# The half tile of a graph-attention layer as rows in pairs, and a neighbourhood-attention layer's projections spread evenly: one Trainium2 core

## The chip, the cores and the metric

The kernel runs as one program on one core of one Trainium2 chip. The metric is the device time of an execution in microseconds: the median of several runs, three for the kernel before.

## The reference, cut to what matters

The input is four images of 56 x 56 tokens with 256 channels, in float32. Four layers follow each other; each computes `x = x + layer(groupnorm(x))`. Layer 0 is attention of 8 heads over a 7 x 7 neighbourhood, layer 2 the same with two dilations and a position bias, layer 3 attention in shifted 7 x 7 windows. Layer 1 is attention of every token to every other of its image, with a kernel that is symmetric since `W_adj` is used by its diagonal:

```python
xn = x / jnp.maximum(jnp.linalg.norm(x, axis=-1, keepdims=True), EPS)
A = jnp.einsum('bnc,cc,bmc->bnm', xn, W_adj, xn)
A = jnp.exp(5.0 * (A - jnp.max(A, axis=-1, keepdims=True)))
A = A * (1.0 - jnp.eye(n, dtype=A.dtype))
A = A / jnp.maximum(jnp.sum(jnp.abs(A), axis=-1, keepdims=True), EPS)
rowsum = jnp.sum(A, axis=-1, keepdims=True)
xW = jnp.einsum('bnc,dc->bnd', x, W_aff)
AxW = jnp.einsum('bnc,dc->bnd', jnp.einsum('bnm,bmc->bnc', A, x), W_aff)
diff = rowsum * (xW + b_aff) - AxW      # then layer norm and leaky relu
```

An image has 3136 tokens, which is 24 tiles of 128 and a rest of 64.

## The kernel before, in words

The four layers run one after the other, each over all four images; activations stand in DRAM between them, with channels on partitions. [...] In layer 1 the order of PE's instructions is the order of the program; the order on the other engines there, and on all engines in layer 0, is made by the framework's scheduler.

**Layer 0** (`layer0`, L1139). An image is read in 7 chunks of 8 rows (448 tokens), so there are 28 chunks. `prepare` (L1173) normalises a chunk on DVE and issues a later chunk's load; `project_rows` (L1187) makes six steps of it: two of values (PE, eviction on DVE, then a store of v to DRAM by SP), two of keys and two of queries (PE, eviction on ACT). The attention goes in 32 blocks of 7 rows, each of four column tiles (`pair`, L1219): PE computes logits of 4 heads at a time on 32-row strips (L1071), DVE and POOL apply masks, ACT the exponential, POOL adds the two halves of the keys (L1091), PE multiplies by v and by ones on 32-column strips (L1100), and DVE divides. `project_out` (L1269) follows one block later. `stream` (L1282) hands out the waiting steps, seven a chunk (six of projection and one `prepare`), among the blocks: chunks 0 and 1 are projected before the first block (L1311 to L1317), and after block `r` a total of `min(182, (7 * (7 * r + 12)) // 8)` steps is done (L1295). All 182 are handed out by block 28.

**Layer 1** (`layer1`, L1331). The rest of 64 tokens is the 25th tile, filled with zeros to 128 (`NB` is 25, L1343 and L1344). `tokens` (L1346) prepares a chunk of up to four tiles: a load, normalising, lengths (PE, L1368), `xW` in `xw` (PE, L1381; with -1 in an added column, which yields the row sum), unit-length tokens in `xnT` (PE L1389, DVE L1391). As A is symmetric before it is divided, only tile pairs with `i >= j` are computed. A unit is row `j` and up to four tiles `i`: `logits` (PE L1409, one matmul of up to 512 columns for each half of the channels; exponential on ACT, L1412; POOL clears the diagonal, L1414), `transposed` (PE L1423 into `ps_t`, copy on ACT, L1426), `products`. There each tile gives a product by column into one of the two banks of `ps_v` (PE L1442), which DVE copies (row 0, L1444) or adds (L1446) to `acc[:, i]`, and a product by row, accumulated in PSUM, `ps_o` (PE L1437). An image has 91 units. After a row, `finish` (L1465) adds `acc` and `ps_o` and applies the layer norm with a chain of operations on DVE and POOL; its `add` (L1491) transposes the result on PE, adds it to the residual and stores a full chunk.

The main loop (L1545) emits for unit k: a small step, the transposes of k, the logits of k + 1, a small step, the products of k. Small steps are the parts of `tokens` for the next image and the `add`s, each due after a number of tiles. `replace` (L1539) starts a chunk of the next image as soon as its tiles are no longer used: chunks 0 to 4 at rows 6, 10, 14, 18 and 22, chunk 5 at row 24, chunk 6 (the rest) at row 0 of the next image. `there` (L1533) emits at once what the next logits need.

Of the kernel before, what the change touches and what calls it, by code (L numbers as in the profile page):

```python
# [830 lines left out]
def direct_blocks(ctx: ExitStack, tc: tile.TileContext, d: dict, watch):  # L831
# [307 lines left out]
    def layer0(early, big, pool, brief):  # L1139
# [142 lines left out]
        def stream():  # L1282
            n = NIMG * NCH
            rows = []
            for c in range(2, n):
                rows += lazily(project_rows, c, 6)
                rows.append(lambda c=c: prepare(c + 1) if c + 1 < n else None)
            look_at = {}
            for b in range(NIMG - 1):
                for i in range(NCH):  # L1290
                    look_at.setdefault(NB0 * b + min(i // 2 + (b == 0), 3), []).append((b + 1) * NCH + i)
            gone = 0
            for r in range(NIMG * NB0):
                b, g = divmod(r, NB0)
                to = min(len(rows), (7 * (7 * r + 12)) // 8)  # L1295
                steps, gone = rows[gone:to], to
                steps += [lambda i=i: first_look(i) for i in sorted(looks)]
                steps.append(lambda r=r: [load(i, looks, "xs") for i in look_at.get(r + 1, [])])
                for i in range(3 if g > 3 or g == 0 else 0):
                    steps.insert(2 * i, step_stats)  # L1300
                if r:
                    steps += table[:3]
                    if len(table) in (1, 2, 3):
                        steps.append(tables.close)
                    del table[:3]
                    at = (len(steps) + 1) // 2
                    steps[at:at] = project_out(r - 1)
                attns[r] = pool.tile([P, CC, BT], FP, tag="attn", name="attn0")
                yield from spread([pair(r, t) for t in range(NTC)], steps)

        for r in range(3):  # L1311
            prepare(r)
            if r == 0:
                load(3)
            if r < 2:
                for step in project_rows(r):
                    step()  # L1317
        check_sizes(pool)
        tables = ExitStack()
        both = [tables.enter_context(tc.tile_pool(name=f"t{n}", bufs=n, side="right", reuse_waits="tile")) for n in (1, 2)]  # L1320
# [7 lines left out]

    def layer1(early, big, pool, brief):  # L1331
        NB = -(-T // P)
        real = lambda i: min(P, T - i * P)
        nonlocal m_bufs
        m_bufs, ps_a = 1, ps_m
        w_aff = weight(early, "waff", C)
        acc = big.tile([P, NB, C + 1], FP, name="acc")
        xnT = big.tile([P, CC, NB * P], FP, name="xnT")
        xw = big.tile([P, NB, C + 1], FP, name="xw")
        offd = big.tile([P, P], FP, name="offd")  # L1340
        nc.vector.tensor_scalar(offd, ident, -1.0, 1.0, ALU.mult, ALU.add)
        nc.vector.memset(xw[:, :, C:], -1.0)
        nc.vector.memset(xw[T % P:, NB - 1, :], 0.0)  # L1343
        nc.vector.memset(xnT[:, :, T:], 0.0)  # L1344

        def tokens(b, c, ps_a=ps_m):  # L1346

            tiles = range(4 * c, min(4 * c + 4, NB))
            n = sum(real(t) for t in tiles)
            k, m = real(tiles[0]), len(tiles)  # L1350
            box = {}

            def load():
                x = early.tile([P, CC, 512], FP, tag="x", name="x1")
                nc.sync.dma_start(out=x[:, :, :n], in_=tokens_of(1, b, 4 * c * P, n))
                x1 = box["x"] = early.tile([P, CC, 512], FP, tag="xn", name="xn1")
                sq = box["sq"] = early.tile([P, CC, 512], FP, tag="sq", name="sq", bufs=1)
                for h in range(CC):
                    normalise(x1[:, h, :n], x[:, h, :n], known(1, b), h)
                nc.scalar.activation(sq[:, :, :n], x1[:, :, :n], AF.Square)  # L1360
# [25 lines left out]
            def unit_length():  # L1386

                pm = ps_a()
                nc.tensor.matmul(pm[:, :n].rearrange("p (m k) -> p m k", k=k), lhsT=ones[:k, :], rhs=box["dg"][:k, :m, :k],  # L1389
                                 start=True, stop=True)  # L1390
                nc.vector.tensor_tensor(xnT[:, :, 4 * c * P:4 * c * P + n], box["x"][:, :, :n],  # L1391
                                        pm[:, :n].rearrange("p (o k) -> p o k", o=1).to_broadcast([P, CC, n]), ALU.mult)

            return [load, lengths] + [lambda i=i: values(i) for i in range(0, m, 2)] + [unit_length]

        xd, out, xr = {}, {}, {}

        def scaled(j):

# [4 lines left out]
        def logits(b, j, first, last):  # L1404

            n = (last - first) * P
            s = psum_tile("s", 2)
            for h in range(CC):
                nc.tensor.matmul(s[:, :n], lhsT=xd[j][:, h, :], rhs=xnT[:, h, first * P:last * P],  # L1409
                                 start=(h == 0), stop=(h == CC - 1))  # L1410
            e = pool.tile([P, 512], FP, tag="e", name="e1", bufs=3)
            nc.scalar.activation(e[:, :n], s[:, :n], AF.Exp, scale=5.0)  # L1412
            if first == j:
                nc.gpsimd.tensor_tensor(e[:, :P], e[:, :P], offd, ALU.mult)  # L1414
            return e

        def transposed(b, j, first, last, e):
            at = pool.tile([P, 512], FP, tag="at", name="at1")
# [10 lines left out]
        def products(b, j, first, last, e, at):  # L1429
# [10 lines left out]
            def by_column(i):  # L1440
                pv = psum_tile("v", 2)
                nc.tensor.matmul(pv[:, :C + 1], lhsT=e[:, col(i)], rhs=xw[:, j, :], start=True, stop=True)  # L1442
                if j == 0:
                    nc.vector.tensor_copy(acc[:, i, :], pv[:, :C + 1])  # L1444
                else:
                    nc.vector.tensor_tensor(acc[:, i, :], acc[:, i, :], pv[:, :C + 1], ALU.add)  # L1446

            rows = list(range(first, last))
            if first == j:
# [5 lines left out]
            for i in rows:  # L1455
                by_row(i)

        def residual(b, c):

            if (b, c) not in xr and c < NCH:  # L1460
# [3 lines left out]

        def finish(b, j):  # L1465

            n = real(j)
            y = pool.tile([P, C + 1], FP, tag="y", name="y", bufs=5)
            u = pool.tile([P, C], FP, tag="u", name="u")
            rd = pool.tile([P, 1], FP, tag="rd", name="rd")  # L1470
            nc.gpsimd.tensor_tensor(u[:n], xw[:n, j, :C], baff[:n], ALU.add)
            if j:
                nc.vector.tensor_tensor(y[:n], out[j][:n, :C + 1], acc[:n, j, :], ALU.add)
            else:
                nc.vector.tensor_copy(y[:n], out[j][:n, :C + 1])
            nc.vector.reciprocal(rd[:n], y[:n, C:])
            y = y[:n, :C]
            nc.vector.scalar_tensor_tensor(y, y, rd[:n], u[:n], ALU.mult, ALU.add)
# [12 lines left out]
            def add():  # L1491
# [5 lines left out]
                while t0 < j * P + n:  # L1497
# [2 lines left out]
                    x = residual(b, c)  # L1500
                    xv = x[:, :, t0 - c * CH:t1 - c * CH]
                    nc.vector.tensor_tensor(xv, xv, pt[:, :, t0 - j * P:t1 - j * P], ALU.add)
                    if t1 == (c + 1) * CH:
                        add_stats(2, b, c, x)
                        nc.sync.dma_start(out=tokens_of(2, b, c * CH, CH), in_=x)
                    t0 = t1
# [1 line left out]

        NC4 = -(-NB // 4)
        units = [(b, j, i, min(i + 4, NB)) for b in range(NIMG) for j in range(NB) for i in range(j, NB, 4)]
        turn = iter(range(4 * NC4))
        fresh = [tokens(0, c, lambda: psum_tile(*(("v", 2), ("o", 2), ("t", 1), ("s", 2))[next(turn) % 4])) for c in range(NC4)]
        for c in range(2):
            fresh[c].pop(0)()
        for c in range(NC4):
            for step in fresh[c]:
                step()
            if c + 2 < NC4:  # L1520
                fresh[c + 2].pop(0)()
        scaled(0)
        e = logits(*units[0])
        small, done = [], 0

        def small_step():
# [3 lines left out]
                    return step()  # L1530
            step_stats()

        def there(b, tile):  # L1533

            for item in [a for a in small if a[2] == (b, tile // 4)]:
                small.remove(item)
                item[1]()

        def replace(b, c):  # L1539
            load, *steps = tokens(b, c)  # L1540
            load()
            at = sum(a[2] is not None for a in small)
            small[at:at] = [(done + 8, step, (b, c)) for step in steps]

        for k, w in enumerate(units):  # L1545
            b, j, first, last = w
            if first == j:
                residual(b, j * P // CH)
                residual(b, j * P // CH + 1)
                if b + 1 < NIMG and j % 4 == 2 and j >= 6:  # L1550
                    replace(b + 1, j // 4 - 1)
                if b + 1 < NIMG and j == NB - 1:
                    replace(b + 1, NC4 - 2)
                if b and j == 0:
                    replace(b, NC4 - 1)
            small_step()
            at = transposed(*w, e)
            if k + 2 < len(units) and units[k + 2][1] == units[k + 2][2]:
                scaled(units[k + 2][1])
            if k + 1 < len(units):  # L1560
                there(units[k + 1][0], units[k + 1][3] - 1)
                ahead = logits(*units[k + 1])
            small_step()
            products(*w, e, at)
            done += last - first
            if last == NB:
                small.append((done + 6, finish(b, j), None))
            e = ahead
        for _, step, _ in small:
            step()  # L1570
# [495 lines left out]
```

## Time and profile before

| what | us |
|---|---|
| median of 3 runs (4103.39 to 4105.45) | 4103.79 |
| the profiled execution's own time | 4092.52 |
| its span in the profile | 4090.7 |
| layer 0, to the first matmul of layer 1 | 0 to 809 |
| layer 1, to the first matmul of layer 2 | 809 to 2846 |
| layers 2 and 3 | 2846 to 4091 |
| PE busy | 3889.7 |
| DVE, POOL, ACT busy | 2369.5, 1741.9, 1377.7 |

The profile is of one execution. Its time is the span plus 1.8 us outside of it, and 11.3 us below the median of the runs. PE is TensorE, DVE VectorE, ACT ScalarE, POOL GpSimd, SP the engine that issues nearly all DMAs. A float32 matmul shows as two records. Records of PE overlap[...]; what one costs is the distance from start to start. "Granted clock" is the share of TensorE's full clock that it was given.

### The profile page before, as it was taken

What the parts mean: (1) busy time and instruction counts of PE and PEld (TensorE: products, weight loads), DVE (VectorE), ACT (ScalarE), POOL (GpSimd) and SP (SyncE); (2) the same over time, 40 slices, a digit from 0 to 9 for tenths busy, and PEclk for the clock granted to TensorE, in tenths of its full rate; (3) what the DMA queues carried; (4) which work ended last, traced back from release to release, by engine and by line L of the source; (5) the groups of instructions that cost most, each with busy time, mean ns of one, the idle gap of its engine ahead of it and who ended that gap; (6) DMA issues with size and microseconds to landing.
All of it is one profiled execution on the core that took longest, in us unless ns stands there. A gap on an engine that the chain in (4) does not pass through costs nothing. (4 is left out here: it accounts for less than half of the span.)

```text
span 4090.7 us, 92322 instructions
## 1 busy us (share of the span) xinstructions
PE 3889.7 (95%) x39031; PEld 2778.1 (68%) x39031; DVE 2369.5 (58%) x4445; ACT 1377.7 (34%) x2890; POOL 1741.9 (43%) x1883
## 2 busy tenths in 40 slices
PE   7899999899999999999999999997999999999998
PEld 4566666577777677776777767775676766666665
DVE  6777777634445444454344543444688877666665
ACT  3445555322222122222222212222555555444443
POOL 2576767621123211242112421123677777554544
PEclk9899999899999999999999999998999999999999
DMA  7344333210000100001000000002344443322221
GB/s 259 101 136 126 116 116 104 90 32 10 15 15 24 34 10 15 15 24 34 10 15 15 23 23 9 10 19 108 108 135 124 131 118 111 108 72 73 73 75 63
DMA packets 239986, 275.88 MB, mean 67 GB/s; under 512 B 22342, under 2 KB 231912, under 8 KB 239080
## 3 DMA queue, kind: packets, MB, share of 16 engines
q1 hardware_dynamic: 239274, 269.80, 21.0%
q8 instruction: 309, 5.06, 0.5%
q14 instruction: 115, 0.94, 0.1%
q10 hardware_dynamic: 288, 0.08, 0.0%
HBM read 190.29 MB, written 79.53 MB: 66 GB/s over the span
## 5 line engine op out<-in xcount | busy, mean ns | idle before, releaser
L1446 DVE TENSOR_TENSOR acc<-acc,ps_v 128x257 f32<-128x257 f32 x1104 | 457.7, 421 | 679.2 <-PE ps_v L1442 676.5
L1442 PE MATMUL ps_v<-xw,e 128*128 128x257 f32 x2400 | 666.6, 382 | 27.2 <-DVE acc L1446 17.2
L1437 PE MATMUL ps_o<-xw,at 128*128 128x257 f32 x2400 | 663.2, 380 | 0.0
L1409 PE MATMUL ps_s<-xnT,xd 128*128 128x512 f32 (+3 forms) x1456 | 622.9, 550 | 5.1 <-DVE xnT L1391 5.1
L1442 PEld LDWEIGHTS ps_v<-xw,e 128*128 128x128 f32 x2400 | 445.0, 189 | 193.2 <-issue 91.8
L1426 ACT COPY at<-ps_t 128x512 f32<-128x512 f32 (+3 forms) x360 | 184.8, 513 | 1053.7 <-PE ps_t L1423 1053.7
L1091 POOL TENSOR_TENSOR b<-e 126x336 f32<-126x336 f32 (+5 forms) x512 | 499.7, 997 | 11.6 <-ACT e L1079 3.6
L1437 PEld LDWEIGHTS ps_o<-xw,at 128*128 128x128 f32 x2400 | 455.9, 190 | 65.5
L1402 POOL TENSOR_SCALAR xd<-xnT,vec 128x128 f32<-128x128 f32 x200 | 122.2, 622 | 707.4 <-PE ps_s L1409 705.6
L945 PE MATMUL ps_m<-xn,w_wqkv 128*128 128x392 f32 x1024 | 380.1, 505 | 2.7 <-DVE xr L1729 2.7
L1082 POOL TENSOR_TENSOR e<-e,m0t 126x672 f32<-126x672 f32 (+3 forms) x128 | 239.3, 1870 | 271.1 <-ACT e L1081 229.6
L1409 PEld LDWEIGHTS ps_s<-xnT,xd 128*128 128x128 f32 x1456 | 245.1, 191 | 155.6 <-issue 138.8
L1082 POOL TENSOR_TENSOR e<-e,bias 119x784 f32<-119x784 f32 (+5 forms) x128 | 244.6, 1911 | 202.0 <-ACT e L1081 200.8
L1412 ACT ACTIVATE e<-ps_s 128x512 f32<-128x512 f32 (+3 forms) x364 | 200.8, 552 | 376.7 <-PE ps_s L1409 376.0
L1003 ACT ACTIVATE no<-rs 128x168 f32<-128x168 f32 (+2 forms) x256 | 93.8, 367 | 596.2 <-DVE rs L1694 271.7
L945 PEld LDWEIGHTS ps_m<-xn,w_wqkv 128*128 128x128 f32 x1024 | 189.4, 192 | 126.1 <-ACT pr L1922 17.5
L1100 PEld LDWEIGHTS ps_o<-e,vp 124*32 124x32 f32 (+3 forms) x8192 | 176.9, 111 | 142.3 <-issue 94.8
L1100 PE MATMUL ps_o<-e,vp 124*32 124x112 f32 (+3 forms) x8192 | 239.5, 254 | 6.1 <-POOL e L1082 4.5
L939 DVE TENSOR_SCALAR xn<-x,gst 128x28 f32<-128x28 f32 (+5 forms) x368 | 206.1, 614 | 56.4 <-PE ps_m L945 27.7
L1079 ACT ACTIVATE e<-e 126x672 f32<-126x672 f32 (+5 forms) x256 | 219.5, 857 | 19.2 <-DVE e L1078 6.2
L1694 DVE RECIPROCAL rs<-ps_o 128x196 f32<-128x196 f32 (+2 forms) x128 | 176.0, 1375 | 78.8 <-PE ps_o L1100 78.3
L1032 POOL TENSOR_TENSOR e<-e,m3l 98x784 f32<-98x784 f32 x64 | 118.2, 1847 | 236.1 <-ACT e L1029 236.1
(169 smaller groups left out, 6176.6 us busy)
## 6 DMA issues: line engine op xcount, KB each, us to landing
x<-xr SPq DMA_DIRECT2D x64, 392.0 KB
x<-in_x SPq DMA_DIRECT2D x53, 448.0 KB
xr<-x SPq DMA_DIRECT2D x60, 392.0 KB
x<-x SPq DMA_DIRECT2D x60, 392.0 KB
vd<-v SPq DMA_DIRECT2D x48, 384.0 KB
xr<-in_x SPq DMA_DIRECT2D x32, 392.0 KB
xr<-x SPq DMA_DIRECT2D x28, 448.0 KB
x<-xr SPq DMA_DIRECT2D x28, 448.0 KB
```

The lines of the kernel that those rows point to most:

```text
L939: nc.vector.tensor_scalar(dst, src, gst[:, h, 0:1], gst[:, h, 1:2], ALU.subtract, ALU.mult)
L945: nc.tensor.matmul(pm[:, :n], lhsT=w[:, h, col:col + P], rhs=rhs(h), start=(h == 0), stop=(h == CC - 1))
L1079: nc.scalar.activation(ev, ev, AF.Exp)
L1082: nc.gpsimd.tensor_tensor(parts(ev), parts(ev), w["emask"], ALU.mult)
L1091: nc.gpsimd.tensor_tensor(w["b"][a][:nk, :, :2 * nq].rearrange("p h (i c) -> p h i c", i=2), ev[:, :, :, 0, :], ev[:, :, :, 1, :], ALU.add)
L1100: nc.tensor.matmul(w["o"](k, i)[j * HD:(j + 1) * HD], lhsT=ones[:nk, :HD] if k else v(j, u), rhs=w["b"][j // 2][:nk, j % 2, i * nq:(i + 1) ...
L1409: nc.tensor.matmul(s[:, :n], lhsT=xd[j][:, h, :], rhs=xnT[:, h, first * P:last * P], start=(h == 0), stop=(h == CC - 1))
L1412: nc.scalar.activation(e[:, :n], s[:, :n], AF.Exp, scale=5.0)
L1426: nc.scalar.copy(at[:, sl], pt[:, sl])
L1437: nc.tensor.matmul(out[j][:, :C + 1], lhsT=e[:, col(i)] if i == j else at[:, col(i)], rhs=xw[:, i, :], start=(i == j), stop=(i == NB - 1))
L1442: nc.tensor.matmul(pv[:, :C + 1], lhsT=e[:, col(i)], rhs=xw[:, j, :], start=True, stop=True)
L1446: nc.vector.tensor_tensor(acc[:, i, :], acc[:, i, :], pv[:, :C + 1], ALU.add)
```

## The change

**Layer 1.** The rest is no longer a 25th tile: `NB` is 24, and an image has 84 units of the old kind and three new ones, `(b, None, q)` with q = 0, 1, 2. Such a unit takes the 64 tokens of the rest against the 8 tiles from `8 * q` on. The rest stands twice in its tile (two loads, in its columns 0 to 63 and 64 to 127), so that half `a` of the partitions holds the rest's logits against the four tiles of chunk `2 * q + a`. One exponential and four transposes then serve both halves. The products by column take 64 rows of the array each, those by row 64 columns each, in pairs. The rest's own block is a small matmul more in q = 2. Units q = 0 and 1 stand at the very beginning for image 0, and behind rows 20 and 21 of the image before for the others; q = 2 stands behind row 0 of the image itself. `acc` is copied at first touch and added to later. The rest's scaled tokens are made by POOL once an image (`xdr`), its row products are summed in `racc`, and its `finish` runs after q = 2, with the `add` after the last row. The chunks of the next image are started at rows 3 (the rest), 6, 10, 14, 18, 20 and 22, each after everything of the chunk before it is emitted.

**Layer 0.** Chunk 2 is projected before the first block too, and chunk 3 is normalised there. The remaining 175 steps are handed out evenly over blocks 0 to 30, or sooner where a block needs them.

```diff
-            for c in range(2, n):
+            for c in range(3, n):
...
+            def needed(r):
+                b, g = divmod(min(r + 1, NIMG * NB0 - 1), NB0)
+                last = min(TR * (g + 1) + 3, S)
+                c = next(c for c in range(NCH) if c == NCH - 1 or (c + 1) * CH // P * P >= last * S)
+                k = 7 * (b * NCH + c - 3) + 6
+                return max(min(len(rows), len(rows) * (r + 1) // (NIMG * NB0 - 1)), k)
...
-                to = min(len(rows), (7 * (7 * r + 12)) // 8)
+                to = needed(r)
...
-            if r < 2:
-                for step in project_rows(r):
-                    step()
+            for step in project_rows(r):
+                step()
+        prepare(3)
...
+                if c == NC4:
+                    for h in range(CC):
+                        nc.gpsimd.tensor_scalar_mul(xdr[:, h, :], xnT[:, h, NB * P:], adj[:, h:h + 1])
...
+        def rest_logits(q):
+            s = psum_tile("s", 2)
+            for a in range(2):
+                for h in range(CC):
+                    nc.tensor.matmul(s[a * REST:(a + 1) * REST, :], lhsT=xdr[:, h, a * REST:(a + 1) * REST],
+                                     rhs=xnT[:, h, (2 * q + a) * 512:(2 * q + a + 1) * 512], start=(h == 0), stop=(h == CC - 1))
+            e = pool.tile([P, 512], FP, tag="e", name="e1", bufs=3)
+            nc.scalar.activation(e, s, AF.Exp, scale=5.0)
...
+        def rest_products(b, q, e, own, at):
+            po = psum_tile("o", 2)
+            for i in range(4):
+                pv = [psum_tile("v", 2) for a in range(2)]
+                for a in range(2):
+                    half = slice(a * REST, (a + 1) * REST)
+                    nc.tensor.matmul(pv[a][:, :C + 1], lhsT=e[half, i * P:(i + 1) * P], rhs=xw[half, NB, :], start=True, stop=True)
+                for a in range(2):
+                    add_up(b, 8 * q + 4 * a + i, pv[a], (nc.vector.tensor_copy, nc.scalar.copy)[a])
+                for a in range(2):
+                    nc.tensor.matmul(po[a * REST:(a + 1) * REST, :C + 1], lhsT=at[:, i * P + a * REST:i * P + (a + 1) * REST],
+                                     rhs=xw[:, 8 * q + 4 * a + i, :], start=(i == 0), stop=(i == 3 and (a == 1 or own is None)))
+            if own is not None:
+                nc.tensor.matmul(po[:REST, :C + 1], lhsT=own, rhs=xw[:REST, NB, :], start=False, stop=True)
...
+        for b in range(NIMG):
+            if b == 0:
+                units += [(b, None, q) for q in range(2)]
+            for j in range(NB):
+                units += [(b, j, i, min(i + 4, NB)) for i in range(j, NB, 4)]
+                if j == 0:
+                    units.append((b, None, 2))
+                if b + 1 < NIMG and 0 <= j - 20 < 2:
+                    units.append((b + 1, None, j - 20))
...
+                if j in (3, 6, 10, 14, 18, 20, 22):
+                    replace(b + 1, {3: NC4, 20: 4, 22: 5}.get(j, j // 4 - 1))
```

## Prediction

> **What bounds the kernel now.** I read the page first (PE 3889.7 us busy of 4090.7, 95%), then the windows by stage, then PE's timeline inside a stage, then the waits of single lines. The windows below give the length of a stretch, then busy time of PE, weight loads, DVE, ACT and POOL, the granted clock, and the DMA share:
>
> ```profile
> 39.12:199.97 160.85, 137.39 (x1819) 85.46 (x1818) 123.37 (x204) 61.31 (x145) 75.39 (x60) 0.87 0.54 157
> 635.24:714.48 79.24, 79.06 (x1417) 54.33 (x1413) 63.20 (x89) 44.82 (x108) 60.77 (x49) 1.00 0.33 104
> 742.37:757.68 15.31, 12.88 (x333) 9.53 (x329) 13.38 (x18) 7.52 (x16) 13.15 (x12) 1.00 0.28 89
> 757.68:777.51 19.83, 16.35 (x332) 11.47 (x329) 13.47 (x18) 8.01 (x17) 15.28 (x13) 0.83 0.30 94
> 849.49:1291.04 441.55, 438.77 (x1916) 326.43 (x1915) 183.63 (x474) 94.34 (x172) 85.62 (x136) 1.00 0.04 14
> 1291.04:1344.04 53.00, 45.07 (x203) 33.24 (x203) 30.72 (x91) 9.97 (x21) 29.71 (x47) 1.00 0.14 45
> 1344.04:1354.70 10.66, 10.66 (x32) 8.02 (x33) 2.09 (x7) 1.75 (x3) 5.08 (x7) 0.52 0.01 2
> 1354.70:1403.02 48.32, 45.54 (x206) 33.20 (x205) 20.79 (x54) 9.59 (x18) 6.14 (x10) 1.00 0.17 50
> ```
>
> The reader is to see four regimes. Layer 1 (809 to 2840) is bound by PE alone: 438.77 of 441.55 us in image 0. Only around the end of an image does PE idle, 7.9 + 2.8 us here, and after the first end it runs 10.7 us at half clock. Layer 0's blocks 24 to 27 (635 to 714) are PE-bound as well; its blocks 29 and 30 (742 to 778), which have no projections left, are not, and block 30 has a clock of 0.83. Blocks 0 to 4 (39 to 200) lose to a clock of 0.87 and to waits. Layers 2 and 3 are not touched.
>
> PE's timeline (start, length, line, count) prices each operation by the distance of starts, since the lengths overlap:
>
> ```profile
> 1002.09 1.88 PE L1409 MATMUL ps_s<-xnT,xd 128*128 128x512 f32 x4
> 1003.81 1.03 PE L1442 MATMUL ps_v<-xw,e 128*128 128x257 f32 x4
> 1004.68 0.60 PE L1437 MATMUL ps_o<-xw,at 128*128 128x257 f32 x2
> 1005.11 0.60 PE L1442 MATMUL ps_v<-xw,e 128*128 128x257 f32 x2
> 1007.28 0.60 PE L1423 MATMUL ps_t<-ident,e 128*128 128x128 f32 x4
> 1007.72 0.61 PE L1409 MATMUL ps_s<-xnT,xd 128*128 128x128 f32 x4
> ```
>
> A matmul is two records. Logits of four tiles take 1003.81 - 1002.09 = 1.72 us, so 0.43 a tile and 0.86 for one of the two 512-column matmuls; a product of 257 columns 0.433; a transpose 0.44 / 4 = 0.109.
>
> [...]
>
> ```profile
> 313.62 0.97 PE L1100 MATMUL ps_o<-e,vp 124*32 124x112 f32 x32
> 314.41 0.57 PE L1100 MATMUL ps_o<-b,ones 124*32 124x112 f32 x16
> 314.91 1.12 PE L1071 MATMUL ps_s<-q,kI 32*126 32x84 f32 x32
> ```
>
> 32 records of 112 columns take 0.79 us, 25 ns each, where 112 columns alone need 0.217 x 112/257 = 0.094. No run shows two halves of 64. [...] over a change, starts here lie 0.09 to 0.13 us further apart than the streaming explains (16 records from 314.41 need 0.38 us; the next starts after 0.50). [...]
>
> **The change, part by part.**
>
> *Half tile, removed per image.* Tile 24 leaves all 25 rows: 25 logits tiles x 0.43 = 10.8, 24 transposes x 0.109 = 2.6, 24 column and 25 row products x 0.433 = 10.4 + 10.8. Sum 34.6 us of PE, all on the path.
>
> *Added per image.* Three units, each with two 512-token chunks on the two 64-partition halves.
> Logits: 4 matmuls a unit x 0.86 = 3.44 if they run one after another, 1.72 if fully in pairs. They stand in the order a0h0, a0h1, a1h0, a1h1[...], so I take three lengths, 2.58, and 0.3 for the changes of shape: 3 x 2.9 = 8.6. Transposes: 12 x 0.109 = 1.3.
> Products: a round is a pair into ps_v (64 rows) and a pair into ps_o (64 columns). If both run in pairs, that is 2 x 0.433, plus two changes of shape at 0.1, plus weight loads that a change leaves uncovered, some 0.15 (first records after a change last 0.02 to 0.10 longer than their fellows): 1.22. [...] The banks of ps_v allow about as much: first result 0.60 after the start, then DVE's copy and ACT's side by side, then the hand-over:
>
> ```profile
> L1446 DVE TENSOR_TENSOR acc<-acc,ps_v 128x257 f32<-128x257 f32 x1104 | 457.7, 421 | 679.2 <-PE ps_v L1442 676.5
> ...
> L954 ACT COPY xw<-ps_m x21: 365/587/588, 1058.7 to 2400.8; 128x512 f32<-128x512 f32 x18, 64x256 f32<-64x256 f32 x3
> ```
>
> 0.60 + 0.42 + some 0.15 = 1.2; ACT's 256 columns (365 ns) are shorter. I take 1.25 for the eight rounds of q = 0 and 1. In q = 2 both are adds on DVE, one after the other: 0.60 + 0.84 + 0.15, so 1.65 for four rounds. Sum 10.0 + 6.6 = 16.6, and 0.9 for the own block. Added 8.6 + 1.3 + 16.6 + 0.9 = 27.4, so 7.2 less an image, **29 us in four**. Bounds: fully serial 11.2 + 1.3 + 12 x 2.08 + 0.9 = 38.4, which is 15 us more in four images; logits in full pairs too, 39 us less.
>
> *Ends of images.* Two units of the next image go behind rows 20 and 21, with some 9 us of PE and little DVE work each, and the 25th finish leaves the end. Who is late there is DVE, queued behind POOL's share of finish:
>
> ```profile
> 1344.04 0.85 PE L1442 MATMUL ps_v<-xw,e 128*128 128x257 f32 x2 [2.96 <-DVE mv L1483]
> ```
>
> Idle gaps add up to 11.8 us at the second and third end, and to 10.7 plus 5.1 of lost clock at the first. I leave 5 at each: **21 us less** (bounds 10 and 33). What is late next is the same DVE queue, behind rows 22 and 23. The last end has no next image and stays. The tokens of the next image are spread differently (rows 3, 6, 10, 14, 18, 20, 22); their PE work is the same, and it stays ahead of its use, so nothing. One DMA more an image on SP's queue, at a DMA share of 0.04 here: nothing.
> *Start of layer 1.* The first unit needs chunk 6 and then POOL's two scalings (604 ns each) before PE can begin: **2 us more**. Layer 1: 48 less.
>
> *Layer 0, start.* A chunk in the prologue takes 39.12 - 29.50 = 9.6 us:
>
> ```profile
> 29.50 3.62 PE L982 MATMUL ps_m<-w_wv,xn 128*128 128x256 f32 x16
> ...
> 39.12 1.02 PE L1071 MATMUL ps_s<-q,kE 32*95 32x112 f32 x32
> ```
>
> Blocks 0 to 4 hand out 35 steps before and 28 after, one chunk less, 9.5 us of PE at full clock and 11 at 0.87. With it its v store and the load of chunk 5 move up on SP's queue, its evictions on ACT, and the normalising of chunk 3 on DVE, which isn't full there (123 of 161). Net 1 us less; bounds 5 less, and 10 more if other waits set these blocks.
> *Layer 0, blocks 5 to 30.* Steps handed out in blocks 5 to 28 go from 147 to 135; at 9.5 / 7 = 1.36 us a step that is 16.3 us. Blocks 29 and 30 take six each, 8.1 us: PE has 12.9 + 8.1 = 21 us there, in place of 15.3 and 19.8, so 6.9 more. Net 9 less (bounds 3 and 15; the gain is what blocks 29 and 30 idle now). Later projections also keep the clock up there. Layer 0: **10 less**.
>
> Sum 58 us less: from the profiled execution, 4092.5 (span 4090.7), 4034.5; from the median, 4103.8, which stands 11.3 above it, 4046.
>
> **Rivals.**
> *Pairs run one after another* (for: no record of 64-wide pairs here; against: quads overlap at 25 ns). The half tile then costs 15 more, the ends give 18 (longer units, more cover), 2 at the start, 10 from layer 0: 11 less, 4093.
> *Rest units stall in DVE's queue: slower.* At the ends each ps_v pair needs DVE at once, and DVE stands in order behind operations that wait for POOL; one such wait is 2.96 us above. Six units there have 24 rounds; at 3 us each 72 come on top: 4046 + 72 = 4118. It turns the sign from 2.4 us a round. Against it: in the whole kernel column products waited 51.5 us for DVE's adds and 20.2 for such operations, 101 times among 1200.
> *Layer 0 gives nothing back*, the prologue's 9.6 us stay: 48 - 10, 38 less, 4066.
>
> **How the numbers follow.** Main case 0.60 (4019 to 4069), layer 0 giving nothing 0.10, serial pairs 0.17, stalls 0.13. About 0.2%, 8 us, is what a measurement can tell from no change. Faster by more: 0.60 + 0.10 + 0.10 of the serial case = 0.80; within: 0.06 of serial, 0.03 of stalls, 0.09; slower 0.11. The range runs from 4016 (all bounds good) to 4094, where it takes in the serial case's better half.
>
> **What would show it.** Right: ps_v records of 64*128 and ps_o records of 128*64 starting in twos a few ns apart, rounds of 1.2 to 1.7 us; 7 us less from one image's first row to the next; gaps at the ends near 5 us; blocks 29 and 30 at some 21 us, the first attention at 49. Wrong: pairs 0.43 us apart (serial), rounds over 2.4 us waiting for DVE (stalls), blocks 0 to 4 still 160 us (layer 0).

## The result, and the profile after

The changed kernel takes 4079.5 us (median of five runs, 4075.0 to 4086.2); the kernel before 4103.8 (4101.4 to 4109.1). The ratio is 0.9940, 95% interval 0.9925 to 0.9954: 24 us faster, where 58 were forecast. The profiled execution took 4082.7, its span is 4080.9. The two profiled executions are only 9.8 us apart (span 4090.7 before), since that of the kernel before lies 11.3 under its median and this one 3.2 above its own.

Where the time went is read from windows of the two profiles, cut at the same instructions. Here is layer 1 (first matmul of its lengths to the first of layer 2), before. The columns are the window's length, then busy time of PE, weight loads, DVE, ACT and POOL, the granted clock, DMA share, GB/s:

```profile
809.15:2845.88 2036.73, 1976.45 (x8729) 1475.31 (x8728) 891.82 (x2337) 423.00 (x780) 492.61 (x764) 0.99 0.06 20
```

and after, with layers 2 and 3 behind it:

```profile
812.95:2833.84 2020.89, 1952.65 (x8681) 1419.13 (x8681) 886.10 (x2318) 419.39 (x784) 492.82 (x764) 0.98 0.07 21
2833.84:4080.90 1247.06, 1200.74 (x18854) 831.15 (x18854) 882.66 (x1227) 584.73 (x1244) 746.60 (x714) 0.98 0.33 103
```

Layer 0 ends 3.8 us later (812.95 for 809.15), layer 1 is 15.8 shorter, and layers 2 and 3, which weren't touched, are 2.2 longer. PE idles 2020.9 - 1952.7 = 68.2 us in layer 1, 8 more than before (60.3), though it has less to do. Its busy time holds lost clock too: where the trace records half clock, half of the busy time under it is counted as lost, 7.7 us before and 30.1 after. In the changed kernel the eight logits records of a rest unit start within 1.35 us at full clock (from 1326.57 on) and within 2.63 under half clock (from 1347.11 on). What remains is PE's work at full clock:

| layer 1, us | length | work | idle | lost clock |
|---|---|---|---|---|
| before | 2036.7 | 1968.7 | 60.3 | 7.7 |
| after | 2020.9 | 1922.5 | 68.2 | 30.1 |
| difference | -15.8 | -46.2 | +7.9 | +22.4 |

The work fell by more than forecast; 30 us of it came back as waits and lost clock. Three profiles of the experiments below repeat one of these two layers unaltered, and tell what of this is firm:

| layer 1, us | length | work | idle | lost clock |
|---|---|---|---|---|
| as before, in the kernel with layer 0 alone changed | 2041.7 | 1968.7 | 60.5 | 12.6 |
| as changed, in the kernel with layer 1 alone changed | 2017.7 | 1923.0 | 68.1 | 26.7 |
| as changed, in the kernel with six steps a block | 2014.5 | 1923.5 | 68.4 | 22.6 |

Work and idle time repeat within 1 us. The lost clock doesn't, so its rise is 10 to 22 us, and what came back is 18 to 30.

These are the changed kernel's blocks 0 to 4 of layer 0, blocks 29 and 30, the middle of image 0, and the first end of an image (first exponential of row 19 to that of row 3 of the next image):

```profile
41.21:196.64 155.43, 133.51 (x1807) 81.86 (x1806) 122.00 (x206) 60.39 (x141) 74.89 (x60) 0.87 0.55 158
...
740.02:763.29 23.27, 22.27 (x365) 14.74 (x360) 14.82 (x21) 11.87 (x28) 15.26 (x12) 1.00 0.32 100
763.29:779.12 15.83, 12.99 (x333) 9.56 (x329) 13.34 (x19) 7.18 (x16) 11.00 (x10) 1.00 0.28 82
986.92:1309.84 322.92, 319.68 (x1415) 239.66 (x1414) 143.07 (x372) 69.53 (x128) 78.32 (x122) 1.00 0.06 17
1309.84:1488.35 178.51, 169.19 (x757) 115.56 (x756) 78.18 (x207) 35.48 (x69) 44.72 (x69) 0.95 0.08 25
```

The last two windows cut at the same rows in the kernel before:

```profile
952.05:1294.69 342.64, 340.55 (x1501) 254.90 (x1500) 148.95 (x384) 73.04 (x134) 75.60 (x118) 1.00 0.05 15
1294.69:1462.58 167.89, 157.18 (x683) 116.32 (x682) 73.42 (x199) 32.91 (x61) 47.33 (x73) 0.97 0.10 29
```

The middle of an image is 19.7 us shorter, nearly all of it busy time: the half tile left it. The end, where three rest units now stand (two behind rows 20 and 21, one behind the next image's row 0), is 10.6 longer, idles 9.3 us (10.7 before), and its clock is 0.95.

Pairs do run together. PE's timeline of the changed kernel at the first unit (start, length, line, shape, records):

```profile
867.25 0.70 PE L1479 MATMUL ps_v<-xw,e 64*128 64x257 f32 x4
...
868.47 0.73 PE L1479 MATMUL ps_v<-xw,e 64*128 64x257 f32 x4
```

Four records of 257 columns, a pair, take the place of two: a round, which is a pair into ps_v and a pair into ps_o, is 868.47 - 867.25 = 1.22 us.

### The profile page after: what moved, and what is told of

Same layout as the page of the kernel before. It is cut to its first block, busy times and chain, and to the rows that moved or that the text cites. A ratio compares the mean times of both kernels' runs of the same rounds, so it can differ in the third digit from the quotient of the medians.

```text
span 4080.9 us, 92234 instructions
## 1 busy us (share of the span) xinstructions
PE 3871.6 (95%) x38983; PEld 2726.9 (67%) x38983; DVE 2363.5 (58%) x4427; ACT 1374.6 (34%) x2894; POOL 1739.7 (43%) x1883
## 3 DMA queue, kind: packets, MB, share of 16 engines
q1 hardware_dynamic: 240362, 270.06, 21.4%
## 4 chain that ended last, share of the span: by engine, by line
PE 47%; DVE 4%; POOL 2%; issue 1%; DMA 0%; ACT 0%; SPq 0%; POOLq 0%; DVEq 0%; ACTq 0%
PE ps_m L945 12%; PE ps_o L1512 6%; PE ps_s L1428 6%; PE ps_v L1517 6%; PE ps_o L1100 3%; PE ps_m L962 3%; PE ps_s L1071 3%; PE ps_o L1040 2%; PE ps_m L982 2%; PE ps_t L1498 1%; PE ps_s L1025 1%; DVE rs L1789 1%; DMA x<-x 0%; PE ps_m L1396 0%; DVE xn L939 0%
## 5 line engine op out<-in xcount | busy, mean ns | idle before, releaser
L1517 PE MATMUL ps_v<-xw,e 128*128 128x257 f32 x2208 | 613.1, 382 | 19.7 <-DVE acc L1440 18.0
L1512 PE MATMUL ps_o<-xw,at 128*128 128x257 f32 x2208 | 609.0, 379 | 0.0
L1428 PE MATMUL ps_s<-xnT,xd 128*128 128x512 f32 (+3 forms) x1344 | 571.1, 547 | 0.0
L1517 PEld LDWEIGHTS ps_v<-xw,e 128*128 128x128 f32 x2208 | 408.6, 189 | 171.1 <-issue 80.4
L1501 ACT COPY at<-ps_t 128x512 f32<-128x512 f32 (+3 forms) x332 | 170.0, 512 | 997.4 <-PE ps_t L1498 997.2
L1512 PEld LDWEIGHTS ps_o<-xw,at 128*128 128x128 f32 x2208 | 419.2, 190 | 59.9
L1428 PEld LDWEIGHTS ps_s<-xnT,xd 128*128 128x128 f32 x1344 | 225.5, 191 | 134.8 <-issue 126.2
L1431 ACT ACTIVATE e<-ps_s 128x512 f32<-128x512 f32 x336 | 185.4, 552 | 332.6 <-PE ps_s L1428 331.1
L939 DVE TENSOR_SCALAR xn<-x,gst 128x28 f32<-128x28 f32 (+5 forms) x368 | 202.4, 605 | 76.5 <-PE ps_m L945 40.1
```

Of the source, the lines that this page charges most:

```text
L939: nc.vector.tensor_scalar(dst, src, gst[:, h, 0:1], gst[:, h, 1:2], ALU.subtract, ALU.mult)
L1512: nc.tensor.matmul(out[j][:, :C + 1], lhsT=e[:, col(i)] if i == j else at[:, col(i)], rhs=xw[:, i, :], start=(i == j), stop=(i == NB - 1))
```

## Experiments

A ratio is to runs of the kernel before on the same chip, whose median was 4103.4 us for the first four kernels, 4089.5 for the one with the pairs taken apart and the very last, and 4092.9 for the other four; so ratios are compared, not times.

### Each layer alone

Layer 0 of the one kernel with layer 1 of the other; the prologue of layer 0 goes with it:

```diff
-            for c in range(3, n):
+            for c in range(2, n):
...
-                to = needed(r)
+                to = min(len(rows), (7 * (7 * r + 12)) // 8)
```

Layer 1 alone:

> Layer 1 as changed, layer 0 as before. Theory: the whole gain is layer 1's and layer 0's change costs some 4 us: layer 0 ends at 809 us as before, layer 1 takes 2021 as in the changed kernel, so about 28 us less than before, 4076. Rival, by which layer 0's change does bring the 10 us that were forecast and what follows is disturbed by something else: 4090 or more.

Measured: 4077.8, ratio 0.9938 (0.9919 to 0.9958). Layer 0 alone, the reverse:

> Layer 0 as changed, layer 1 as before. Theory: nothing is gained, since from block 15 on the floor (what the next block needs) hands out the steps, not the even share: layer 0 ends at 813, the whole takes 4108. Rival (the forecast): 4094.

Measured: 4101.8, ratio 1.0005 (0.9993 to 1.0016). The whole gain is layer 1's; layer 0's change is worth nothing that can be measured, neither the 10 us that were forecast nor a clear loss.

### The third rest unit in the middle of row 1

```diff
-                units += [(b, j, i, min(i + 4, NB)) for i in range(j, NB, 4)]
-                if j == 0:
-                    units.append((b, None, 2))
+                row = [(b, j, i, min(i + 4, NB)) for i in range(j, NB, 4)]
+                if j == 1:
+                    row.insert(3, (b, None, 2))
+                units += row
```

What it is to avoid stands in the changed kernel's timeline at image 0's third unit, which follows row 0 and its `finish`:

```profile
917.59 0.72 POOL L1563 TENSOR_TENSOR y<-y,bc 128x256 f32<-128x256 f32 x1
...
918.35 0.66 DVE L1564 SCALAR_TENSOR_TENSOR y<-y 128x256 f32<-128x256 f32 x1 [1.30 <-POOL y L1563]
918.93 0.74 DVE L1440 TENSOR_TENSOR acc<-acc,ps_v 128x257 f32<-128x257 f32 x2
...
919.39 0.70 PE L1479 MATMUL ps_v<-xw,e 64*128 64x257 f32 x2 [1.60 <-DVE acc L1440]
```

DVE's next operation is a step of `finish` that waits 1.30 us for POOL. The additions that would free the banks of ps_v stand behind it, and PE idles 1.60 us. At 920.9 half clock begins.

> The changed kernel with the third rest unit of an image moved from behind row 0 into the middle of row 1, where no finish has just been queued on DVE. Theory (DVE's queue makes the pair into ps_v wait, and the idle time halves the clock): the waits of 1.6 to 2.1 us and the half clock of 3.4 to 6.8 us behind them go in all four images, 14 us less, 4066. Rival (the half-array pairs with their changes of shape are themselves too little work for the clock): the half clock moves along with the unit, 8 us less at most, 4072 or more.

Measured: 4052.1, ratio 0.9881 (0.9862 to 0.9901), more than expected. Layer 1 is 1997.4 us, with 58.7 idle and 15.8 of lost clock: 9.5 and 14.3 less than in the changed kernel (of lost clock 6.8 to 14.3, by which of the three profiles of the changed layer 1 it is set against). The unit in its new place:

```profile
931.05 0.70 PE L1479 MATMUL ps_v<-xw,e 64*128 64x257 f32 x4
...
932.27 1.03 PE L1479 MATMUL ps_v<-xw,e 64*128 64x257 f32 x4
...
933.81 0.70 PE L1479 MATMUL ps_v<-xw,e 64*128 64x257 f32 x4
```

No wait, no half clock, though it is the same unit with both additions on DVE: rounds of 1.22 and 1.54 by turns. So the pairs as such don't halve the clock here; the half clock went when the waits did.

### Both first-touch copies of a rest unit on ACT

```diff
-                    add_up(b, 8 * q + 4 * a + i, pv[a], (nc.vector.tensor_copy, nc.scalar.copy)[a])
+                    add_up(b, 8 * q + 4 * a + i, pv[a], nc.scalar.copy)
```

The changed kernel at the first end, where unit q = 0 follows row 20:

```profile
1335.66 0.53 DVE L1561 TENSOR_SCALAR y<-y,mv,rstd 128x256 f32<-128x256 f32 x1 [1.59 <-POOL rstd L1560]
1336.11 0.41 DVE L1443 COPY acc<-ps_v 128x257 f32<-128x257 f32 x1
...
1336.58 0.70 PE L1479 MATMUL ps_v<-xw,e 64*128 64x257 f32 x4 [1.59 <-DVE acc L1443]
```

It is the same chain by another step: POOL's rstd, DVE's step of `finish`, the copy behind it, PE.

> The changed kernel with the first-touch copies of the rest units (q = 0 and 1) all on ACT, none on DVE. Theory (DVE's queue): the waits of 1.6 + 0.4 to 0.8 + 1.6 us at each of three ends go, and with them most of the half clock there (13.7, 13.7 and 3.4 us, half of it lost), 20 to 25 us less, 4057. Rival (the pairs themselves halve the clock): 11 us less, 4068. If ACT's two copies in series, 0.75 us, are too slow for the round of 1.22 us, rounds become 1.6 us and the gain shrinks by 0.4 x 32 = 12 us.

Measured: 4063.1, ratio 0.9900 (0.9881 to 0.9918), between the two. Layer 1 is 2003.3: idle 56.7, lost clock 22.4, so 11.5 and 7.7 less.

### Both edits

> The changed kernel with both edits that were tried singly: the third rest unit in the middle of row 1, and both first-touch copies of a rest unit on ACT. Theory (DVE's queue behind `finish` is what holds the rest units, and each short wait of PE there also brings half clock): the waits that the kernel with the moved unit still has at the three ends, 1.60 + 0.78 + 1.62 us each, 12 in all, go, and half clock at the ends falls from 20 to about 10 us, 5 us of time; 17 less than the kernel with the moved unit, so 4035. Rival (pairs of half-array matmuls halve the clock by themselves): the ends keep their half clock and gain 12 at most from the waits, of which ACT's own queue takes part: 4043 or more.

Measured: 4037.8, ratio 0.9868 (0.9851 to 0.9885), 55 us less than the runs of before beside it. That is short of the 68 expected, but layer 1 did what the theory says: 1979.9 us, 17.5 less than with the third unit moved alone. Idle is 46.3, lost clock 9.0. The shortfall lies outside of layer 1: in this profile the untouched layers 2 and 3 take 10 us more than in that of the kernel with the third unit moved (1246.2 for 1236.0), 8 of them in lost clock. The list of waits shows what went; first the changed kernel (engine, result and line that waits, what for: us in total, times, longest):

```profile
PE ps_v L1479 <- DVE acc L1443: 11.6, 9, 1.6
...
PE ps_v L1479 <- DVE acc L1440: 8.5, 8, 2.1
```

The 11.6 us in nine waits are the six units at the ends, the 8.5 in eight waits the third units. These 20.1 us are missing in the kernel with both edits; there only weight loads wait, beside PE's work:

```profile
PEld ps_v L1479 <- ACT acc L1443: 9.3, 24, 0.4
...
PEld ps_v L1479 <- DVE acc L1440: 4.6, 12, 0.4
```

and its first end is

```profile
1302.90:1469.12 166.22, 163.06 (x757) 113.47 (x756) 74.97 (x199) 37.68 (x76) 44.59 (x69) 0.99 0.09 27
```

with 3.2 us idle in place of 9.3. Half clock remains for 3.4 us each at two of the three ends, with no wait in the 14 us ahead of it: it starts after a rest unit that 16 records of one column follow (the lengths of the next image's tokens). This doesn't speak for the rival: the kernel of "The pairs taken apart", below, whose products don't run in pairs, has the same 3.4 us at all three of its ends, behind the same 16 records.

### Rest units 0 and 1 away from the end

On top of both edits:

```diff
+                if b + 1 < NIMG and j in (13, 19):
+                    row.insert(len(row) - 1, (b + 1, None, j // 19))
                 units += row
-                if b + 1 < NIMG and 0 <= j - 20 < 2:
-                    units.append((b + 1, None, j - 20))
```

> As the kernel with both edits of layer 1, and the rest units q = 0 and 1 of the next image away from the end: q = 0 in row 13, q = 1 in row 19, each in front of the row's last unit. This asks what their cover at the ends is worth. Theory (they cover waits there, as my forecast had it): the ends go back to the idle time of the kernel before, 11 us each in place of some 5, and to its half clock: 18 more in idle time, so 4053. Rival (what the units cover at an end is no more than what their own short rounds cost in waits and clock there): within 5 of the kernel with both edits, 4030 to 4040.

Measured: 4072.9, ratio 0.9951 (0.9937 to 0.9964): 35 us more than with both edits. Layer 1 is 2019.9: idle 67.7 (21.4 more), lost clock 19.8 (10.8 more), and 8 of longer work that I didn't place; the last two, which the expectation had left out, are why it is 20 us above the 4053. What PE waits for at the first end now are above all the additions and the next image's token steps; both kinds of wait stood there before the change too:

```profile
PE ps_v L1517 <- DVE acc L1440: 2.5, 2, 1.3
...
PE ps_m L1396 <- DVE rn L1385: 1.9, 1, 1.9
```

So the cover at the ends is real and of the size that my forecast gave it, 21 us in three ends. It shows as less idle time only where the rest units have no waits of their own.

### The pairs taken apart

On top of both edits, with the same matmuls:

```diff
                 for a in range(2):
                     half = slice(a * REST, (a + 1) * REST)
                     nc.tensor.matmul(pv[a][:, :C + 1], lhsT=e[half, i * P:(i + 1) * P], rhs=xw[half, NB, :], start=True, stop=True)
-                for a in range(2):
                     add_up(b, 8 * q + 4 * a + i, pv[a], nc.scalar.copy)
-                for a in range(2):
                     nc.tensor.matmul(po[a * REST:(a + 1) * REST, :C + 1], lhsT=at[:, i * P + a * REST:i * P + (a + 1) * REST],
```

> The kernel with both edits of layer 1, and in the rest's products the two halves no longer next to each other: column product of half 0, row product of half 0, column product of half 1, row product of half 1. The same matmuls, but no two of one shape are neighbours. Theory (a pair costs one matmul's time only because both halves stream at once): a round of a unit goes from 1.22 us to four lengths of 0.433 and four changes of shape at 0.1, 2.13; 48 rounds make 44 us; 11 less than before in place of 55 less, a ratio near 0.997. Rival (the banks of ps_v and the evictions set the round anyway, or halves of different shape overlap as well): under 15 us more, a ratio of 0.987 to 0.990.

Measured: 4089.0, ratio 0.9996 (0.9986 to 1.0006). Its timeline:

```profile
868.56 0.70 PE L1479 MATMUL ps_v<-xw,e 64*128 64x257 f32 x2
869.19 0.65 PE L1481 MATMUL ps_o<-xw,at 128*64 128x257 f32 x2
...
870.97 0.70 PE L1479 MATMUL ps_v<-xw,e 64*128 64x257 f32 x2
```

A single matmul takes as long as a pair did, 0.60 us on average, and a round 2.41, more than the 2.13 expected. Layer 1 grows by 52.9 us, its work by 51.2. This order also changes shape four times a round where pairs change it twice. As an estimate: if a matmul on half the array streams as long as a whole one, 0.43 us, a change costs 0.60 - 0.43 = 0.17; then 0.34 of the 1.19 us a round are the added changes, and the rest, 0.85, is the lost overlap. For a round in pairs the same figures give 2 x 0.60 = 1.20, where 1.22 is measured. Together they are worth as much as the whole gain: the kernel with both edits and this order is no faster than the kernel before. Its half clock at the first end follows these records, without a wait:

```profile
1349.48 1.95 PE L1383 MATMUL ps_m<-ones,sq 128*128 128x1 f32 x16
...
1352.19:1355.60 3.41, 3.41 (x10) 1.12 (x7) 0.00 (x0) 1.19 (x3) 1.57 (x2) 0.50 0.00 0
```

### Layer 0 with six steps a block

In the changed kernel:

```diff
-                return max(min(len(rows), len(rows) * (r + 1) // (NIMG * NB0 - 1)), k)
+                return max(min(len(rows), 6 * (r + 1)), k)
```

> The changed kernel, layer 0 handing out six steps in each block up to block 28, in place of the larger of an even share and what the next block needs (which gives 10 in block 23, none in block 26 and 7 in blocks 27 to 29). Layer 1 as in the changed kernel. Theory (the jumps are what takes away layer 0's gain): layer 0 ends at about 805 in place of 813, 4072. Rival (layer 0's projections cost PE the same wherever they stand, and its waits and its clock move with them): layer 0 ends at 811 to 815, 4080.

Measured: 4076.0, ratio 0.9958 (0.9945 to 0.9970); layer 0 ends at 813.6. My theory, that the uneven numbers of steps take away layer 0's gain, falls. Stretches of layer 0 in the three profiles, up to block 0, blocks 0 to 4, blocks 5 to 28, and to the end; in brackets work, then idle and lost clock together:

| us | to block 0 | blocks 0 to 4 | blocks 5 to 28 | to the end |
|---|---|---|---|---|
| before | 39.1 | 160.8 | 542.4 (493.5 + 48.9) | 66.8 |
| after | 41.2 | 155.4 | 543.4 (486.9 + 56.5) | 72.9 |
| six a block | 40.1 | 162.4 | 547.8 (490.4 + 57.4) | 63.3 |

All of layer 0 has 677, 679 and 676 us of work, and 132, 134 and 137 of idle time and lost clock. Each distribution moves both from block to block; none takes them away.

### The best version

The two edits of layer 1, and for image 0 the rest's tokens prepared third:

```diff
+        fresh.insert(2, fresh.pop())
         for c in range(2):
             fresh[c].pop(0)()
```

First with six steps a block in layer 0:

> As the kernel with both edits of layer 1, and two more: for image 0 the rest's tokens are prepared third, so that the scaled rest is ready when the first unit needs it; and layer 0 hands out six steps a block. Theory: the start of layer 1 loses its gaps of 2.27 and 1.40 us and some 10 us of half clock, 8 less; layer 0 is 8 less; so 4035 - 16 = 4019. Rival: the start of layer 1 only shifts its wait to the load of the rest, and layer 0's distribution is worth nothing: 4035.

Measured: 4031.9, ratio 0.9851 (0.9836 to 0.9865), which is near the rival's 4035 and not the theory's 4019: only the start of layer 1 gave something. Then with layer 0 of the kernel before:

> Layer 0 of the kernel before, layer 1 of the changed kernel with its three edits (third unit in the middle of row 1, first-touch copies on ACT, the rest's tokens prepared third for image 0). Theory (layer 0's change is worth nothing in either form): as the kernel with six steps a block and the same layer 1, which had a ratio of 0.985: 0.984 to 0.987. Rival (six steps a block gave part of the gain): 0.988 or more.

Measured: 4027.5, ratio 0.9839 (0.9816 to 0.9861), the fastest of all. The intervals of the two overlap. In the changed kernel the first rest unit began like this:

```profile
855.76 0.53 PE L1404 MATMUL ps_t<-dg,ones 128*128 128x128 f32 x2 [2.27 <-POOL dg L1387]
857.68 4.46 PE L1450 MATMUL ps_s<-xnT,xdr 128*64 128x512 f32 x8 [1.40 <-POOL xdr L1410]
```

Eight records took 4.46 us there, at half clock after two waits; in the best version, where the unit follows the tokens' last matmul with no wait shown,

```profile
849.08 1.94 PE L1441 MATMUL ps_s<-xnT,xdr 128*64 128x512 f32 x8
```

they take 1.94. Layer 1 is 1974.3 there, 5.6 less than with the two edits alone, of which 1.0 is idle time and 4.3 lost clock.

## Why the prediction was right or wrong

**The direction was right, the size was not**: 24 us in place of 58. The result lies in the stated range, but only since that had room for the other cases: the main case's own, 4019 to 4069, misses it. One of its terms was too small and two didn't come at all, and these errors partly cancelled.

**Half tile (29 less): too small, 46 less, beyond its good bound of 39.** I had left each pair a part of its serial time. It takes none: logits 1.9 us a unit in place of 2.9, rounds of 1.22 in place of 1.25, and 1.22 and 1.54 by turns in place of 1.65 for q = 2. Three lengths for a unit's four logits matmuls were one too many: in the changed kernel the eight records from 1326.57 on start in four twos, 13 to 14 ns apart, so all four matmuls shared their time. Why they do isn't shown. The records of a pair of products start 6 to 7 ns apart, as forecast. Three units then cost 5.6 + 1.3 + 8 x 1.22 + 4 x 1.38 + 0.9 = 23.1, so 34.6 - 23.1 = 11.5 less an image and 46 in four, as measured. The 0.35 a round that my sum added for changes of shape and weight loads fits as a whole: from 867.25 on, the steps of a round start 0.32, 0.31, 0.27 and 0.32 us after one another, where records of whole 257-column matmuls start 0.22 apart (from 1328.98 on), and the estimate from the unpaired kernel gives 0.17 us for every change, 0.34 a round. How it divides between the two was not shown. The "some 0.15" for the hand-over of a bank was my estimate: DVE's copy starts 0.04 us behind the end of its matmul there, ACT's 0.12, and the matmul that takes the bank next 0.05 to 0.06 behind the copy.

**Ends of images (21 less): the step that failed.** I wrote "I leave 5 at each". The cover that I counted was there: taking it away costs 21.4 us of idle time. What I didn't set against it is what the rest units need there: DVE at once, in a queue whose head waits for POOL. The third rival named this mechanism, but I priced it only as the whole (24 rounds at 3 us), gave it a chance, and left it out of the main case's sum. At the ends and at the third units it took 17 waits of up to 2.1 us, 20.1 us in all, and half clock came with seven of the ten that lasted 1.6 us or more. Over the three ends idle time went from 32.2 to 28.7 us, 3.5 less, while lost clock rose from 5.1 to 21.4. So in place of 21 less the ends gave 13 more (8 to 15 more with the other three profiles of these two layers). "What is late next is the same DVE queue, behind rows 22 and 23" named the right queue, at the wrong rows: it was late at the rest units themselves. The third unit's place behind row 0 had no line in my sum at all, and moving it alone is worth 23.5 us of layer 1. Nor had the middles of the images and the last end, which idle 7 us more (25.7 before, 32.7 after).

**Start of layer 1 (2 more): 2 to 5.** Up to row 3, the start lost 2.4 us to idle time and 1.7 to the clock before, 6.8 and 7.5 after; with the third unit moved it is 4.8 and 4.3. So in these profiles 5 us belong to the start and 5 to that unit. Only the idle time is firm, 2.4 and 2.0 of them: in the other two profiles of the changed layer 1 its start lost 1.7 and 2.5 us to the clock.

**Layer 0 (10 less): wrong, 4 more in the profile and nothing in the medians.** The 4 are no firm figure either: the changed layer 0 ends between 807.7 and 813.2 us in the profiles that have it. Three terms:
- Start, 1 less: 3.3 less. The first block starts 2.1 later, not 9.6, since the scheduler doesn't keep a whole chunk ahead of it (72 records of projection matmuls stand there in place of 60), and blocks 0 to 4 are 5.4 shorter.
- Blocks 5 to 28, 16.3 less: 1.0 more. I took an even share for granted. Working out `needed` gives 139 steps there, not 135, since what the next block needs exceeds the even share in most blocks from 16 on; a step is worth (493.5 - 486.9) / (147 - 139) = 0.8 us of work, not the 1.36 that I read off the prologue, whose waits were in it. These 6.6 us came back as 7.5 of idle time and lost clock.
- "Blocks 29 and 30 take six each", 6.9 more: they take seven and one, and 4.0 more. The clock is 1.00 in both, where block 30 had 0.83. Block 31 and the way to layer 1's first matmul, for which I had nothing, add 2.2.

Handing out the same number in each block gives no more, so the unevenness is not the cause. Which wait sets the floor of 132 to 137 us of idle time and lost clock stays open. In layer 0 PE waits longest for DVE's `attn` before (19.0 us), for DVE's `e` in the other two (24.3 and 21.8).

**Rivals.** Serial pairs: no. The unpaired kernel isn't quite that case, as its shapes change at every matmul of a round and its logits matmuls stand as in the changed kernel; its layer 1 has 51 us more work than with both edits and 7 more than before, where the rival had 15 more than before. Layer 0 giving nothing: yes. Stalls: yes in kind, without turning the sign. The six units at the ends waited 11.6 us, where the rival had 72, and lost clock came on top. What I set against it was misread: the 51.5 and 20.2 us count waits of weight loads too; PE itself waited 17.2 and 8.9 us there, 26 times.

**A slip in the sum**: the good bounds add up to 90 us, so the range should have begun at 4014, not 4016. Nothing hangs on it.

**Layers 2 and 3**: 2.2 longer; their own profiles of unchanged code differ by up to 13 us in this set.

## What to carry to other kernels

A unit that is put into another's idle time as cover brings its own demands with it: look at the head of every queue that it needs in that place, and price the wait in the main sum, not only as a disaster. Place such work away from the in-order chain of the step before it (in the middle of a row), or give its evictions to an engine that doesn't run that chain. Where a change says "evenly", work out its function block by block before believing the word. And where a loss is lost clock, see in a second profile whether it repeats before building on it.

## What the runs showed of the hardware

- In each of the twelve profiles, half clock between 813 and 2760 us (layer 1 without its last end) comes in stretches of 3.4, 6.8, 10.2 and 13.7 us, whose begins and ends lie whole multiples of 3.41 us apart (within 0.01 us in the profiles of the kernel before and of the changed one). Cut at these distances, the windows at full clock in which PE idled 1.8 us or more were followed by half clock in 28 cases of 29 (3 of 4 in those two profiles), those with 1.3 to 1.8 us in 21 of 68 (7 of 17), the others in 10 of 6643 (none of 1095), nine of which held the whole 1.8 us of one-column records. That is a count; what sets the clock was not shown. The kernel before has a wait of 2.96 to 2.98 us at each of its three ends. At the first end it lies in one window, and half clock follows; at the second and the third a border between two windows divides it, and none follows. The windows at the first and the second end:

```profile
1341.05:1344.46 3.41, 0.45 (x3) 0.39 (x3) 2.45 (x11) 0.00 (x0) 1.95 (x3) 1.00 0.00 0
...
1853.05:1856.47 3.42, 1.86 (x11) 1.70 (x12) 1.78 (x7) 0.00 (x0) 2.62 (x5) 1.00 0.00 0
```

  In layer 1, both edits took away 21.9 us of idle time and 21.1 of lost clock; that is a sum of two profiles, not the price of every wait.
- Two float32 matmuls of 257 columns on halves of 64 rows, or of 64 columns, took the time of one: 0.61 us for a pair (a round of 1.22 in the changed kernel), 0.60 for a single one (a round of 2.41 in the unpaired kernel). A change between the shapes 64 x 128 and 128 x 64 costs some 0.17 us by the estimate above (the unpaired kernel's 0.60 less the 0.43 of a whole 257-column matmul), over a third of such a matmul; what it consists of was not shown.
